# A graph layer on one core: the second layer's results turned by VectorE, another read order for the edges, shifted tables, five more picks

## The chip, the cores and the metric

The kernel runs on one core of a Trainium2 chip. The metric is the device time of one execution in microseconds (us). Before the change three runs took 1513.1 (median), 1511.35 and 1513.92 us. A separate execution was recorded by the profiler; all durations below come from it.

## The reference

There are 6250 nodes with 64 features each, and 200000 edges sorted by their target `dst`. For every edge a small network makes nine weights from 32 attributes; they scale nine further attributes, and the source node's features are combined with them. The results are summed per target node, scaled and shifted by a function of `node_vec`, added to `x`, and normalised.

```python
w = jax.nn.silu(edge_attr @ W1 + b1) @ W2 + b2
h_src = features[src]
msg = jnp.einsum('ef,em,fmg->eg', h_src, edge_sh * w, W_tp)
agg = jax.ops.segment_sum(msg, dst, num_segments=N) / jnp.sqrt(jnp.float32(AVG_DEG))
emb = jax.nn.silu(c_noise[:, None] @ Wn1 + bn1) @ Wn2 + bn2
gamma, beta = jnp.split(emb, 2, axis=-1)
return agg * (1.0 + gamma) + beta
```

The final step is `_layernorm(x + ...)` over the 64 features.

## The kernel before

**Tiling.** The edges stand in 1563 tiles of 128, one edge per partition, and in 98 groups of 16 tiles (`KB`; the last has 11). Because the edges are sorted, the 128 edges of a tile reach at most 7 neighbouring nodes (`W`). A fallback for other inputs stands behind the main path and is not run.

**Three ways to fetch the source rows.** The features of an edge's source node go into a tile `hs` of the group, and come from one of three places. Most tiles are fetched by an indirect DMA that GpSimd issues (`gather`, L99), one per tile. The last 3 or 4 tiles of each group are "picked" by TensorE. One tile of each fourth group is read row by row by DMAs of the SP queue (L115). That makes 1173 gathers, 367 picks and 23 tiles by rows.

**A pick** (`pick`, L488 to L511) works on a copy of the whole node table in SBUF, split in two parts of reduced precision: `xs[0]`, rounded, and `xs[1]`, the remainder. Node number 49 p + 7 h + l lies on partition p. For each h, VectorE compares the edges' keys with the partition numbers (`hots`, L485); the one-hot matrix `hot_k[:, h, :]` is the weight operand of two matmuls, one for each part of `xs` (L500, 448 columns: 64 features by 7 values of l). Fourteen of them add up in `px`, a PSUM tile with two buffers. VectorE then keeps the right l (L509, `xm`) and adds over l (L511) into `hs`. A pick can begin only when L509 of the pick before the last has read the buffer it is to use. How many picks a group has is set by `picked`: 4, or 3 where the group's number is a multiple of 4.

**The edge network.** `hidden` (L423) multiplies the attributes by `W1` in two matmuls of 512 columns (L428) into the PSUM tile `p1`, 64 hidden values for two sets of edges on 128 partitions; ScalarE applies silu (L436). `second` (L440) multiplies by `W2` in four matmuls (L445), one for each 128 columns, each into its own 32 partitions of the PSUM tile `p2`; ScalarE adds the bias into `p2s` (L448). There, the weights lie along partitions and the edges along the columns. `weights` (L450) turns this: two TensorE transposes of 128 by 128 (L455), put back into `p2`, then two multiplications by the nine attributes (L461), and one by the one-hots of the target within its window of 7 (L467), which makes `a`.

**Sums.** `windows` (L519) multiplies `hs` and `a` for every tile (L533): 64 features by 9 times 7 sums. Its first matmul in a group waits for all gathers of the group. `project` (L565) multiplies by `W_tp` for two groups at a time (L579); ScalarE copies the result to `rt` (L582), and TensorE turns it (L585); ScalarE and VectorE split it (L553, L554) and VectorE makes place marks (L563). `place` and `bring` (L595, L612) put the sums to their nodes, and `finish` normalises and stores 2 x 128 nodes at a time.

**Order.** It is written out by hand; each engine executes in the program's order. Iteration i issues the gathers of group i + 6, the first pick of group i + 1 with the node work of `nodes` between its matmuls, then `hidden(i + 2)`, `second(i + 1)`, `windows(i)`, `project` in odd iterations, and the rest of the picks. The second pick carries other work between its matmuls: after each pair of matmuls, `pick` calls the next entry of a list, which is built at L675 from `weights(i + 1)` (two entries) and, in odd iterations, from `project` (two empty entries and the turn, L585). `hs` has seven buffers.

**Addresses.** The tiles are laid out in the order in which they are made. Helper `even` rounds small tiles up to 128 bytes, so that all large tiles start at multiples of 64 bytes in a partition. `xs[0]`, `xs[1]` and all one-hot tiles start at multiples of 256.

Of the kernel before, what the change touches and what calls it, by code (L numbers as in the profile page):

```python
# [11 lines left out]
F32R = mybir.dt.float32r  # L12
# [4 lines left out]
P = 128  # L17
N, F, M, D, H, E = 6250, 64, 9, 32, 64, 200000
NJ = 49
# [10 lines left out]
Q = 4  # L30
J = 7
# [19 lines left out]

def picked(g):

    return Q - (g % 4 == 0)


def tiles(g):
# [3 lines left out]
def even(pool, p, n, dt, **kw):  # L61

    per = 32
    return pool.tile([p, -(-n // per) * per], dt, **kw)[:, 0:n]
# [3 lines left out]
def gnn_resnorm_kernel(ctx: ExitStack, tc: tile.TileContext, x, src, dst, dst_row, ea, sh, cn,  # L68
                       w1, b1, w2, b2, wtp, wn1, bn1, wn2, bn2, out):
    nc = tc.nc  # L70
# [6 lines left out]
    w1bd = consts.tile([P, 2 * H], F32)  # L77
# [9 lines left out]
    with ExitStack() as fast:  # L87
# [3 lines left out]
        keep = fast.enter_context(tc.tile_pool(name="keep", bufs=1))  # L91
# [5 lines left out]
        def gather(g):  # L97
            hs[g] = gath.tile([P, KB, F], F32, tag="hs", name=f"hs{g}")
            hs_dma[g] = [nc.gpsimd.indirect_dma_start(  # L99
                out=hs[g][:, t - g * KB, :], out_offset=None, in_=x,  # L100
                in_offset=bass.IndirectOffsetOnAxis(ap=src_i[:, t:t + 1], axis=0))
                for t in range(g * KB + (g in SPG), g * KB + tiles(g) - picked(g))]
# [14 lines left out]
        ident = keep.tile([P, P], F32)  # L117
        ident2 = keep.tile([P, F], F32)
        w2p = keep.tile([P, D], F32)
        b2c = even(keep, P, 1, F32, name="b2c")  # L120
        xs = [keep.tile([P, J, F, J], F32R, name=f"xs{i}") for i in range(2)]
        wi = even(keep, P, W, F32, name="wi")
        nf = keep.tile([P, 2 * P], F32)
        lo = even(keep, P, NBLK, F32, name="lo")
# [20 lines left out]
        def setup(temp):  # L145
# [77 lines left out]
            def keys_first(g, kf, tag):  # L223

                pk_t[g] = psum.tile([P, Q, P], F32, tag=tag, name=f"pk{g}")
                for t in range(picked(g)):
                    c = (g + 1) * Q - picked(g) + t
                    d0 = NBLK * KB + c * P
                    dg = xb.rearrange("p j f -> p (j f)")[:, d0:d0 + P]
                    nc.vector.tensor_scalar(dg, ident, kf[:, c:c + 1], None, op0=ALU.mult)  # L230
                    nc.tensor.matmul(pk_t[g][:, t, :], ones, dg, start=True, stop=True)  # L231
# [26 lines left out]
            pick(0, 0)  # L258
            hots(0, 2, Q)
            hidden(0)  # L260
            keys_first(1, kf, "s")
            hots(1, 0, 1)
# [4 lines left out]
            hots(1, 1, Q)  # L267
            second(0)
            pick(0, 2, [[lambda: None, lambda: None], weights(0)])
            hidden(1)  # L270

            nc.sync.dma_start(dst_i[:, 2 * KB:], dst[:, 2 * KB:])
# [150 lines left out]
        def hidden(g, act=True):  # L423

            e = ea_t.pop(g)
            p1 = psum.tile([P, 2, KB * P // 4], F32, tag="p1", name=f"p1_{g}")
            for i in range(2):
                nc.tensor.matmul(p1[:, i, :], w1bd[i * 64:(i + 1) * 64, :], e[i * 64:(i + 1) * 64, :],  # L428
                                 start=True, stop=True)
            p1_t[g] = p1  # L430
            if act:
                hidden_act(g)

        def hidden_act(g):
            st[g] = work.tile([P, 2, KB * P // 4], F32, tag="st", name=f"st{g}")
            nc.scalar.activation(st[g], p1_t.pop(g), AF.Silu, bias=b1c)  # L436
# [13 lines left out]
        def weights(g):  # L450

            p, v = p2.pop(g), p2s.pop(g)

            def part(i):
                nc.tensor.transpose(p[:, 1, i * P:(i + 1) * P], v[:, i * P:(i + 1) * P], ident)  # L455
                if i == 0:
                    return
                sw = p[:, 0, 0:KB * M].rearrange("p (t m) -> p t m", m=M)
                sh = sh_t.pop(g)
                for i in range(2):  # L460
                    nc.vector.tensor_mul(  # L461
                        sw[:, 8 * i:8 * i + 8].rearrange("p (s c) m -> p s c m", s=2),
                        p[:, 1, i * P:(i + 1) * P].rearrange("p (c q) -> p c q", q=D)[:, :, 0:2 * M]
                        .rearrange("p c (s m) -> p s c m", s=2),
                        sh[:, 8 * i:8 * i + 8].rearrange("p (s c) m -> p s c m", s=2))
                a[g] = work.tile([P, KB, M, W], F32, tag="a", name=f"a{g}")
                nc.vector.tensor_mul(a[g], oh_t.pop(g)[:, :, None, :].to_broadcast([P, KB, M, W]),  # L467
                                     sw.unsqueeze(3).to_broadcast([P, KB, M, W]))

            return [lambda i=i: part(i) for i in range(2)]  # L470

        hot_k = {}

# [162 lines left out]
        with tc.manual_schedule(), tc.tile_pool(name="temp", bufs=1) as temp:  # L636
            setup(temp)

            for i in range(NBLK):
# [26 lines left out]
                if i + 2 < NBLK:  # L666
                    hidden(i + 2)
# [5 lines left out]
                if i % 4 == 1 and i - 1 < NJ:  # L673
                    gate_hidden(i - 1)
                pick(i + 1, 1, [weights(i + 1), turn])  # L675
                for t in range(2, Q):
                    pick(i + 1, t)

            g = NBLK - 1
            second(g)  # L680
            nc.scalar.activation(root, eps, AF.Sqrt)
            pick(g, 1, [weights(g)])
            pick(g, 2)
            sums(g)
# [225 lines left out]
```

## Time and profile before

| What | Value |
|---|---|
| Median of three runs | 1513.1 us |
| Profiled execution, whole | 1512.09 us |
| Span from its first to its last instruction | 1510.2 us |
| TensorE busy | 1459.4 us (97%) |
| VectorE busy | 1152.7 us (76%) |
| ScalarE busy | 514.6 us (34%) |
| GpSimd busy | 1113.2 us (74%) |
| DMA | 96.3 MB, 64 GB/s on average |

A line of the groups reads: source line, engine, operation, the tiles written and read, their shapes, how many; then busy time in total and mean duration of one in ns; then the idle time of that engine just before them, and who ended most of it. Matmuls overlap in the array and their ends are modelled, so a mean duration of 374 ns does not say how far apart they follow each other; their start times do. A line of the timeline reads: start and duration in us, engine, line, operation, tiles, and in brackets the idle time before it with the one who ended it. PE is TensorE, PEld its weight loads, DVE VectorE, ACT ScalarE, POOL GpSimd, SP the engine that issues most DMAs.

### The profile page before, as it was taken

How to read it: one execution, taken by the hardware profiler on the slowest of the kernel's cores; microseconds unless marked ns; L12 is line 12 of the kernel's file. 1: busy time of each engine (PE TensorE's matmuls, PEld its weight loads, DVE VectorE, ACT ScalarE, POOL GpSimd, SP SyncE). 2: the span in 40 equal slices, each digit the busy share in tenths (PEclk: the TensorE clock that was granted, in tenths of full speed). 3: DMA queues.
4: the chain of work that ended last, by engine and by line, in shares of the span. 5: the costliest groups of instructions: out<-in, count | busy, mean ns of one | idle time of the engine just before them, and what ended most of it. 6: DMA issues, size and time to landing. Idle time of an engine off the chain costs nothing.

```text
span 1510.2 us, 34381 instructions
## 1 busy us (share of the span) xinstructions
PE 1459.4 (97%) x10984; PEld 1207.7 (80%) x10984; DVE 1152.7 (76%) x2044; ACT 514.6 (34%) x1326; POOL 1113.2 (74%) x1182
## 2 busy tenths in 40 slices
PE   5899999999999999999999999999999999999996
PEld 3688788878787888787878888788888888888885
DVE  6777877777868777778687788777886877877774
ACT  3333333333423333334233333243342333333342
POOL 7777777777777777777777777777777777777770
PEclk9899999999999999999999999999999999999997
DMA  5422222222222222222222222222222222222210
GB/s 166 97 72 64 72 58 64 55 59 70 65 57 73 58 64 54 69 61 65 54 73 54 60 54 73 60 55 54 71 62 54 72 55 60 70 58 60 72 30 7
DMA packets 90424, 96.30 MB, mean 64 GB/s; under 512 B 36824, under 2 KB 51370, under 8 KB 90234
## 3 DMA queue, kind: packets, MB, share of 16 engines
q1 hardware_dynamic: 52122, 53.89, 12.0%
q0 software_dynamic: 37536, 38.51, 11.6%
q8 instruction: 90, 1.47, 0.4%
q10 hardware_dynamic: 576, 1.61, 0.3%
q14 instruction: 100, 0.82, 0.2%
HBM read 92.17 MB, written 1.73 MB: 62 GB/s over the span
## 4 chain that ended last, share of the span: by engine, by line
PE 84%; DVE 6%; ACT 2%; issue 2%; SPq 2%; POOL 2%; DMA 1%; DVEq 0%; POOLq 0%; ACTq 0%
PE px L500 63%; PE pz L533 6%; PE p L428 5%; PE p L445 3%; PE pt L579 3%; POOL hs L99 2%; SPq L115 1%; PE p L455 1%; ACT L436 1%; DMA hs<-in_x_dram,src_i 1%; ACT st L436 1%; DVE xm L509 1%; PE ps L595 1%; DVE hs L511 1%; PE ps L625 1%
## 5 line engine op out<-in xcount | busy, mean ns | idle before, releaser
L99 POOL DMA_INDIRECT hs<-in_x_dram,src_i x1173 | 1111.9, 948 | 359.5 <-issue 316.9
L500 PE MATMUL px<-xs,hot_k 128*128 128x448 f32 x5138 | 1136.1, 374 | 2.0 <-ACT xs L245 1.3
L500 PEld LDWEIGHTS px<-xs,hot_k 128*128 128x128 f32 x5138 | 929.7, 189 | 93.5 <-DVE xs L246 3.2
L509 DVE SCALAR_TENSOR_TENSOR xm<-li,jl,px 128x448 f32<-128x448 f32 x367 | 248.3, 677 | 231.7 <-PE px L500 231.7
L485 DVE TENSOR_TENSOR hot_k<-pk,nk 128x896 fp32r<-128x896 f32 x367 | 382.7, 1081 | 1.9 <-PE pk L231 1.9
L436 ACT ACTIVATE st<-p,b1c 128x1024 f32<-128x1024 f32 x98 | 109.1, 1114 | 399.6 <-PE p L428 399.3
L511 DVE TENSOR_REDUCE hs<-xm 128x64 f32<-128x448 f32 x367 | 227.6, 620 | 12.6
L543 ACT COPY ztw<-pz 64x140 f32<-64x140 f32 (+1 forms) x780 | 208.6, 267 | 16.5 <-PE pz L533 5.3
L533 PEld LDWEIGHTS pz<-a,hs 128*64 128x64 f32 x3116 | 100.0, 138 | 43.5 <-issue 42.7
L467 DVE TENSOR_TENSOR a<-oh,p 128x1008 f32<-128x1008 f32 x98 | 118.0, 1204 | 3.3
L533 PE MATMUL pz<-a,hs 128*64 128x63 f32 x3116 | 113.4, 225 | 3.0 <-issue 2.0
L428 PE MATMUL p<-ea,w1bd 64*128 64x512 f32 x392 | 111.6, 646 | 0.0
L601 ACT COPY carry<-ps 128x128 f32<-128x128 f32 x48 | 12.8, 266 | 277.2 <-PE ps L595 277.2
L461 DVE TENSOR_TENSOR p<-p,sh 128x72 f32<-128x72 f32 x196 | 47.0, 240 | 59.1 <-PE p L455 27.4
L445 PEld LDWEIGHTS p<-st,w2p 128*32 128x32 f32 x784 | 15.8, 108 | 89.3 <-issue 43.9
L728 ACT ACTIVATE var<-var,eps 128x2 f32<-128x2 f32 (+1 forms) x25 | 7.4, 295 | 207.5 <-DVE var L725 207.5
L445 PE MATMUL p<-st,w2p 128*32 128x256 f32 x784 | 63.1, 393 | 15.4 <-DVE xb L369 7.9
L579 PE MATMUL pt<-ztw,wtc 128*64 128x112 f32 x960 | 55.3, 261 | 2.7 <-ACT st L436 2.5
L479 ACT CAST pk<-kr 128x512 f32<-128x512 f16 (+1 forms) x96 | 54.2, 564 | 1.7 <-DMA kr<-kd 1.7
L455 PE MATMUL p<-ident,p2s 128*128 128x128 f32 x196 | 53.5, 273 | 0.1
L428 PEld LDWEIGHTS p<-ea,w1bd 64*128 64x128 f32 x392 | 29.7, 186 | 29.8 <-issue 26.4
L579 PEld LDWEIGHTS pt<-ztw,wtc 128*64 128x64 f32 x960 | 46.8, 137 | 4.6 <-ACT st L436 4.0
(139 smaller groups left out, 528.5 us busy)
## 6 DMA issues: line engine op xcount, KB each, us to landing
hs<-in_x_dram SPq DMA_DIRECT2D x2944, 0.2 KB
ea<-in_ea_dram SPq DMA_DIRECT2D x48, 512.0 KB
hs<-in_x_dram,src_i POOLq DMA_INDIRECT x1173
kr<-kd SPq DMA_DIRECT2D x48, 256.0 KB
sh<-in_sh_dram SPq DMA_DIRECT2D x49, 144.0 KB
cb<-cn_d SPq DMA_DIRECT2D x12, 128.0 KB
out_dram<-o SPq DMA_DIRECT2D x24, 64.0 KB
dst_i<-in_dst_dram SPq DMA_DIRECT2D x1, 768.0 KB
```

The lines of the kernel that those rows point to most:

```text
L99: hs_dma[g] = [nc.gpsimd.indirect_dma_start(out=hs[g][:, t - g * KB, :], out_offset=None, in_=x, in_offset=bass.IndirectOffsetOnAxis(ap=sr ...
L428: nc.tensor.matmul(p1[:, i, :], w1bd[i * 64:(i + 1) * 64, :], e[i * 64:(i + 1) * 64, :], start=True, stop=True)
L436: nc.scalar.activation(st[g], p1_t.pop(g), AF.Silu, bias=b1c)
L445: nc.tensor.matmul(p2[g][c * D:(c + 1) * D, 0, :].rearrange("p (i e) -> p i e", i=2), w2p, s[:, :, c * P:(c + 1) * P], start=True, stop=True)
L467: nc.vector.tensor_mul(a[g], oh_t.pop(g)[:, :, None, :].to_broadcast([P, KB, M, W]), sw.unsqueeze(3).to_broadcast([P, KB, M, W]))
L485: nc.vector.tensor_tensor(hot_k[g, t], pk_t[g][:, t, None, :].to_broadcast([P, J, P]), nk.unsqueeze(2).to_broadcast([P, J, P]), op=ALU.is_ ...
L500: nc.tensor.matmul(px.rearrange("p f l -> p (f l)"), hot_k[g, t][:, h, :], xs[i][:, h].rearrange("p f l -> p (f l)"), start=(h == 0 and i ...
L509: nc.vector.scalar_tensor_tensor(xm, li[:, None, :].to_broadcast([P, F, J]), jl[:, c:c + 1], px, op0=ALU.is_equal, op1=ALU.mult)
L511: nc.vector.tensor_reduce(hs[g][:, tiles(g) - q + t, :], xm, AX.X, ALU.add)
L533: mm = nc.tensor.matmul(pz[v][v * F:(v + 1) * F, k // 2].rearrange("p m w -> p (m w)"), hsg[:, k0 + k, :], ag[:, k0 + k].rearrange("p m w ...
L543: nc.scalar.copy(z[h * F:(h + 1) * F, 0:5 - h, k0 + v:k0 + n:2, :].rearrange("p m k w -> p k m w"), pz[v][v * F:(v + 1) * F, 0:(n + 1 - v) ...
L579: nc.tensor.matmul(pt[h * F:(h + 1) * F, 0, 0:KW], wtc2[:, c, :], z[h][:, c], start=(c == 0), stop=(c == 4))
```

## The change

It has four parts.

- The two TensorE transposes of a group are replaced by one VectorE transpose, which turns each 32 by 32 block of the 128 by 256 tile by itself. The list of `weights` so has one entry instead of two.
- Block-wise turning leaves an edge in the quarter of the partitions in which its block lay. So that the edges still come out in their places, the first layer reads its 512 columns in another order: its four sets of 128 are read by quarters of 32, first quarters first.
- `xs` becomes one tile with both parts in it, each with a margin of 32 bytes in front. In the built program the parts start at 139296 and 151968, the one-hots at 190976 and every 3584 bytes on.
- `picked` gives 3 picks where the group's number is a multiple of 5: 20 groups instead of 25. There are 372 picks and 1168 gathers.

```diff
 def picked(g):
 
-    return Q - (g % 4 == 0)
+    return Q - (g % 5 == 0)
...
-        xs = [keep.tile([P, J, F, J], F32R, name=f"xs{i}") for i in range(2)]
+        xs_w = keep.tile([P, 2, NJ * F + 32], F32R)
+        xs = [xs_w[:, i, 8:8 + NJ * F].rearrange("p (h f l) -> p h f l", h=J, f=F) for i in range(2)]
...
             for i in range(2):
-                nc.tensor.matmul(p1[:, i, :], w1bd[i * 64:(i + 1) * 64, :], e[i * 64:(i + 1) * 64, :],
+                nc.tensor.matmul(p1[:, i, :].rearrange("p (c t e) -> p c t e", c=4, t=4), w1bd[i * 64:(i + 1) * 64, :],
+                                 e[i * 64:(i + 1) * 64, :].rearrange("p (t c e) -> p c t e", t=4, c=4),
                                  start=True, stop=True)
...
-            def part(i):
-                nc.tensor.transpose(p[:, 1, i * P:(i + 1) * P], v[:, i * P:(i + 1) * P], ident)
-                if i == 0:
-                    return
+            def part():
+                nc.vector.transpose(p[:, 1, :], v)
                 sw = p[:, 0, 0:KB * M].rearrange("p (t m) -> p t m", m=M)
...
-            return [lambda i=i: part(i) for i in range(2)]
+            return [part]
```

## The prediction

> **What bounds the kernel now.** I read the busy times first, then the chain that ended last, then the costliest groups.
>
> ```profile
> PE 1459.4 (97%) x10984; PEld 1207.7 (80%) x10984; DVE 1152.7 (76%) x2044; ACT 514.6 (34%) x1326; POOL 1113.2 (74%) x1182
> ...
> PE 84%; DVE 6%; ACT 2%; issue 2%; SPq 2%; POOL 2%; DMA 1%; DVEq 0%; POOLq 0%; ACTq 0%
> ...
> L99 POOL DMA_INDIRECT hs<-in_x_dram,src_i x1173 | 1111.9, 948 | 359.5 <-issue 316.9
> L500 PE MATMUL px<-xs,hot_k 128*128 128x448 f32 x5138 | 1136.1, 374 | 2.0 <-ACT xs L245 1.3
> ...
> L455 PE MATMUL p<-ident,p2s 128*128 128x128 f32 x196 | 53.5, 273 | 0.1
> ```
>
> TensorE carries 84% of the chain and waits for almost nothing. GpSimd looks idle for a quarter of the span, but 316.9 us of that is "issue": it waits for nobody. The timeline from 1451 us shows what this means.
>
> ```profile
> 1451.62 1.15 PE L533 MATMUL pz<-a,hs 128*64 128x63 f32 x32
> ...
> 1452.38 0.94 POOL L99 DMA_INDIRECT hs<-in_x_dram,src_i  x1 [0.30 <-issue]
> ...
> 1453.21 0.27 PE L455 MATMUL p<-ident,p2s 128*128 128x128 f32 x1
> ...
> 1453.63 0.94 POOL L99 DMA_INDIRECT hs<-in_x_dram,src_i  x1 [0.31 <-issue]
> 1453.73 0.27 PE L455 MATMUL p<-ident,p2s 128*128 128x128 f32 x1
> ...
> 1454.11 0.52 DVE L461 TENSOR_TENSOR p<-p,sh 128x72 f32<-128x72 f32 x2 [1.01 <-PE p L455]
> 1454.66 1.20 DVE L467 TENSOR_TENSOR a<-oh,p 128x1008 f32<-128x1008 f32 x1
> ...
> 1466.52 1.15 PE L533 MATMUL pz<-a,hs 128*64 128x63 f32 x32
> ...
> 1472.36 0.94 POOL L99 DMA_INDIRECT hs<-in_x_dram,src_i  x1 [0.30 <-issue]
> ```
>
> Gathers follow each other every 1.247 us, without a break from about 50 us until the last, 1173rd, one at 1472.36. So there are two chains: TensorE's work, and 1173 gathers in a row. They meet at L533, whose first matmul needs its group's gathers. Group 95's L533 starts at 1466.52; groups 96 and 97 have 13 + 7 gathers, so group 95's last gather ended near 1448.3: TensorE came 18 us later than the gathers. That margin was 30 us at the start and shrank after 800 us.
>
> Two sizes come from start times in the trace. A pick without other work between its 14 matmuls has 13 intervals of 2634 ns in all: 202.6 ns each. A second pick of an odd group, with two L455 transposes inside, has 2960. Its first interval is 311 instead of 203 because it follows L533's small matmuls; that 108 is not the transposes'. They cost 2960 - 2634 - 108 = 218 ns, 109 each. Check: where L585 is added, 3080, so 120 for one more transpose. The 273 ns of the row overlap neighbours.
>
> **What the Trainium skill says.** TensorE: Matmul & The Clock Gate, "Back-to-back issue gap", gives columns / 2.4 + 2.5 ns: 189.2 for 448 columns. The trace, with a granted clock of 1.00 in every stretch from 50 to 1480 us, has 202.6: 13.4 ns more. SBUF — State Buffer, "Who interferes with whom", says that TensorE has two independent read ports, for moving operand and weights, and waits for nobody. It speaks against a gain from addresses, but does not explain the 13.4. Vector Engine (DVE) Microarchitecture Reference, 3.8, says that the block transpose sustains one element per cycle per lane; no transpose of VectorE is in this trace.
>
> **The change, part by part.**
>
> (a) 196 transposes and their weight loads leave TensorE: 98 x 0.218 = -21.4 us on the path.
>
> (b) 98 block transposes come to VectorE. Its rows cost about 156 ns + 1.06 per element (L721: 292 for 128, 224 for 64), so an estimate of 0.43 us, 42 us in all; were each block filled and drained in turn, 0.7. Lower bound is half the elements' time, 0.29. What hides it: VectorE idles 24% of the span, and its waits before L461 (59.1 us) go, 27.4 of them for L455. The tight place is the second pick of every fourth group: there L509 frees its px buffer 0.91 us (median) before TensorE wants it. Minus 0.218 and 0.43 leaves 0.26. Queued behind are the two L461, L467, L554, the marks and L509; the next pick but one waits for L509. Cost 0; at 0.7 still about 0 to 1 us, and 24 x the excess beyond.
>
> (c) The list given to the second pick loses one entry, so L585 comes after 8 matmuls, not 10 matmuls and two transposes: 0.62 us earlier. Its weight load now starts 0.55 to 0.57 us after the copy of rt ended in 12 of 48 cases, 0.78 or more in nearly all others. With 0.06 for the semaphore (L554's end to L595 near the end) about 12 waits of 0.12: +1.5. ACT's copy and VectorE's L554 and marks follow it, earlier than before.
>
> (d) 25 groups had three picks, now 20: five more. TensorE 5 x 14 x 0.2026 = +14.2. VectorE 5 x (1081 + 677 + 620) ns = 12, hidden in idle. GpSimd loses 5 gathers: -6.2 on its own chain, 4 of them (-5.0) by group 95.
>
> (e) L428 reads 16 runs of 32 columns (128 bytes each). No row before does so; L445 reads two runs of 128 at no visible cost. I take 0. Bounds: -1 (no mechanism for more), and +10, at four lost cycles (1.7 ns) for each run in two passes of two matmuls per group: 64 x 1.7 x 98.
>
> (f) In the built program the two xs start at 139264 and 151808 per partition, one-hots at 190720 and every 3584 on, rows inside step by 1792 and 512: both streams always start at a multiple of 256. After: 139296 and 151968 against 190976: always 32 past a multiple of 128. It concerns 372 x 14 = 5208 matmuls, 5.2 us per ns. Bounds: -13.4 ns (the whole excess, -70 us), and on the other side, which no row excludes, as much. The excess is about the same for L595 (256 columns, 119 ns against 109.2), so it goes with the matmul and its 128-column weight load, not with columns: what two colliding reads of the same weights would give. Against it: L579, also at multiples of 64, needs 48 ns for 112 columns per pass, almost no excess, though with 64 weight columns.
>
> **The sum.** TensorE without (f): 1510.2 - 21.4 + 14.2 + 1.5 = 1504.5. GpSimd: group 95's gathers end at 1443.3, land 1.1 to 2.4 later, so L533 can start at 1444.8; TensorE without (f) is there at 1466.5 - 96 x 0.218 (20.9) + 4 x 2.84 (11.3) + 1.5 = 1458.4. The 13.6 between is all that (f) can give: 2.7 ns per matmul, a fifth of the excess. Beyond that, from 1444.8 on: 1510.2 - 1466.5 = 43.7 as before, + 2.8 for group 96's new pick, - 0.4 for two groups' transposes, - 0.3: 1490.6. A span shorter by 19.6. The profiled execution took 1512.1, 1.9 around its span; the median of runs is 1513.1, so 1493.5.
>
> **The cases.** A, 55%: (f) gives 2.7 ns or more, GpSimd's chain sets the end: 1493.5 (1491 to 1496). For it: four fifths of the interval between no gain and the whole excess lie here. B, 14%: a gain below 2.7 ns, which TensorE passes on whole, 5.2 us per ns: 1496 to 1506, 1500.4 at half. C, 18%: the offset does nothing, as the two ports suggest, and one part of the change does not do what it says: 1504.5 + 2.9 = 1507.4, still 5.7 faster. GpSimd then keeps 13.6 us of margin and never shows. D, 13%, the other side: the reads from xs become slower at the new offset. Nothing in the trace speaks for it but that no matmul of this shape was seen there. It decides from 5.7 / 5.2 = 1.1 ns; at 5 ns the time is 1533. I drop VectorE as the bound: it would need 0.26 us beyond 0.43 in one block, and then costs 24 x the rest.
>
> The range 1489.5 to 1508.5 holds A, B and C but for their edges, some 82%; A's own is 1491 to 1496. Less than 0.2% (3 us) can't be told from no change. A, B and C are faster, (e) at its upper bound takes C to the same, D splits: faster 0.86, same 0.05, slower 0.09.
>
> **What would show it.** L500's interval: 200 or less for A, 202.6 for C, above 203.7 for D. L533 waiting for hs gathers at groups 75 to 95, in A only. Last gather near 1466. No L455; VectorE's transpose at 0.43. L428 at 527 ns per matmul. L585's weight load waiting for ACT some 0.1 us. The forecast is wrong if gathers lose their pace of 1.247, if L509 comes late every block, or if the interval doesn't move.

## The result and the profile after

The changed kernel takes 1510.76 us (median of 12 runs, 1508.88 to 1511.82 us); the kernel before, run beside it, 1512.76 (12 runs, 1510.41 to 1514.67). The ratio is 0.9989, with a 95% interval of 0.9980 to 0.9997: 0.5 to 3 us faster, which the prediction's own bound of 0.2% does not tell from no change. 1493.5 was forecast, and 1510.8 lies above the range. The profiled execution has a span of 1507.1 us, 3.1 shorter than before.

From the page of the changed kernel: the busy times, the chain that ended last, and the groups that answer to those shown of before.

```profile
PE 1456.1 (97%) x10858; PEld 1204.8 (80%) x10858; DVE 1202.3 (80%) x2157; ACT 515.3 (34%) x1326; POOL 1108.4 (74%) x1177
...
PE 86%; DVE 6%; SPq 2%; issue 2%; ACT 2%; DMA 1%; POOL 1%; DVEq 0%; POOLq 0%; ACTq 0%
...
L99 POOL DMA_INDIRECT hs<-in_x_dram,src_i x1168 | 1107.2, 948 | 358.0 <-issue 317.2
L500 PE MATMUL px<-xs_w,hot_k 128*128 128x448 f32 x5208 | 1133.0, 371 | 2.4 <-ACT xs_w L246 1.3
...
L461 DVE TENSOR_TENSOR p<-p,sh 128x72 f32<-128x72 f32 x196 | 47.3, 241 | 6.7
```

L455 is gone and 126 matmuls are fewer (196 transposes less, 70 of five more picks), VectorE is busy for 50 us more, and TensorE still fills 97% of the span and carries 86% of the chain. The gathers are five fewer and just as fast. The timeline of the changed kernel at group 44's windows (L533) and the second and third picks of group 45 shows the new order.

```profile
712.24 1.15 PE L533 MATMUL pz<-a,hs 128*64 128x63 f32 x32
...
713.32 6.38 PE L500 MATMUL px<-xs_w,hot_k 128*128 128x448 f32 x30
...
715.08 0.45 DVE L457 STREAM_TRANSPOSE p<-p2s 128x256 f32<-128x256 f32 x1
...
715.56 0.52 DVE L461 TENSOR_TENSOR p<-p,sh 128x72 f32<-128x72 f32 x2
...
717.24 0.67 DVE L509 SCALAR_TENSOR_TENSOR xm<-li,jl,px 128x448 f32<-128x448 f32 x1
```

TensorE now goes through the second pick without a break, and one block transpose of 0.45 us on VectorE stands where two of TensorE stood. The same timeline near the end:

```profile
1461.68 1.15 PE L533 MATMUL pz<-a,hs 128*64 128x63 f32 x32
...
1466.18 0.94 POOL L99 DMA_INDIRECT hs<-in_x_dram,src_i  x1 [0.30 <-issue]
```

Group 95's L533 starts at 1461.7, where its gathers had ended at 1443.4 (96 and 97 take 12 + 7 after them). The margin is still 18 us, so the gathers bound nothing. The forecast had TensorE there at 1444.8.

Where the time went is in the start times of L500 in the trace. The table gives the sum of the 13 intervals between the 14 matmuls of a pick; the first row is a pick without other work in it, and the two others are second picks, which carry the transposes:

```
                        before   after
13 intervals of a pick    2634    2645 ns   (202.6 -> 203.5 per matmul)
second pick, odd group    2960    2761 ns   (-199 = -210 + 11)
second pick, with L585    3080    2873 ns   (-207 = -218 + 11)
```

The matmuls after alternate between 205 ns (with xs part 0) and 202 (part 1). 5208 matmuls x 0.85 ns = 4.4 us. So the sum is -20.5 (96 second picks, freed of the offset's 11 ns) + 14.2 (five picks) + 4.4 = -1.9 us, and the medians show -2.0. That they agree to 0.1 us is luck in part, because single executions differ by more. In the traces the changed kernel is 2.0 us ahead at group 1 (64.4 against 66.4), where f1 below, with the same instructions on other addresses, is at 66.6. And at group 60 TensorE waits once for VectorE, 2.94 us in the kernel before and 3.01 in the changed one. The changed kernel's trace shows a granted clock of 0.50 for the next 3.4 us, where the kernel before has 1.00, and it loses some 1.2 us.

In eleven of the eighteen runs below (e1 to e5, g1 to g4, h5 to h7) TensorE was held at half its clock for long stretches (the kernel before took 2442 to 2533 us beside them), so only their intervals at full clock are read, and no times.

### The profile page after: what moved, and what is told of

Same layout as the page of the kernel before. It is cut to its first block, busy times and chain, and to the rows that moved or that the text cites. A ratio compares the mean times of both kernels' runs of the same rounds, so it can differ in the third digit from the quotient of the medians.

```text
span 1507.1 us, 34188 instructions
## 1 busy us (share of the span) xinstructions
PE 1456.1 (97%) x10858; PEld 1204.8 (80%) x10858; DVE 1202.3 (80%) x2157; ACT 515.3 (34%) x1326; POOL 1108.4 (74%) x1177
## 4 chain that ended last, share of the span: by engine, by line
PE 86%; DVE 6%; SPq 2%; issue 2%; ACT 2%; DMA 1%; POOL 1%; DVEq 0%; POOLq 0%; ACTq 0%
PE px L500 66%; PE pz L533 6%; PE p L429 5%; PE p L447 3%; PE pt L579 3%; SPq L115 2%; DMA hs<-in_x_dram,src_i 1%; PE ps L595 1%; DVE xm L509 1%; ACT L438 1%; PE ps L625 1%; POOL hs L99 1%; ACT st L438 1%; DVE hs L511 1%; DVE hot_k L485 1%
## 5 line engine op out<-in xcount | busy, mean ns | idle before, releaser
L500 PE MATMUL px<-xs_w,hot_k 128*128 128x448 f32 x5208 | 1133.0, 371 | 2.4 <-ACT xs_w L246 1.3
L500 PEld LDWEIGHTS px<-xs_w,hot_k 128*128 128x128 f32 x5208 | 954.4, 188 | 95.4 <-DVE xs_w L247 3.4
L509 DVE SCALAR_TENSOR_TENSOR xm<-li,jl,px 128x448 f32<-128x448 f32 x372 | 251.6, 676 | 221.6 <-PE px L500 219.1
L485 DVE TENSOR_TENSOR hot_k<-pk,nk 128x896 fp32r<-128x896 f32 x372 | 387.6, 1081 | 2.1 <-PE pk L232 2.1
L511 DVE TENSOR_REDUCE hs<-xm 128x64 f32<-128x448 f32 x372 | 230.7, 620 | 12.8
L533 PEld LDWEIGHTS pz<-a,hs 128*64 128x64 f32 x3116 | 100.8, 139 | 44.0 <-issue 39.4
L533 PE MATMUL pz<-a,hs 128*64 128x63 f32 x3116 | 114.2, 226 | 3.2 <-issue 2.4
L429 PE MATMUL p<-ea,w1bd 64*128 64x512 f32 x392 | 110.6, 641 | 0.0
L447 PEld LDWEIGHTS p<-st,w2p 128*32 128x32 f32 x784 | 15.8, 108 | 89.2 <-issue 44.7
L447 PE MATMUL p<-st,w2p 128*32 128x256 f32 x784 | 63.3, 395 | 15.2 <-DVE xb L370 7.6
L579 PE MATMUL pt<-ztw,wtc 128*64 128x112 f32 x960 | 55.2, 261 | 2.4 <-ACT st L438 1.8
L429 PEld LDWEIGHTS p<-ea,w1bd 64*128 64x128 f32 x392 | 29.5, 184 | 30.1 <-issue 26.0
L450 ACT ACTIVATE p2s<-p,b2c 128x256 f32<-128x256 f32 x98 | 45.7, 466 | 15.6 <-PE p L447 15.6
L579 PEld LDWEIGHTS pt<-ztw,wtc 128*64 128x64 f32 x960 | 46.8, 137 | 4.3 <-ACT st L438 3.0
```

The costliest lines, as they stand in the source:

```text
L429: nc.tensor.matmul(p1[:, i, :].rearrange("p (c t e) -> p c t e", c=4, t=4), w1bd[i * 64:(i + 1) * 64, :], e[i * 64:(i + 1) * 64, :].rearra ...
L447: nc.tensor.matmul(p2[g][c * D:(c + 1) * D, 0, :].rearrange("p (i e) -> p i e", i=2), w2p, s[:, :, c * P:(c + 1) * P], start=True, stop=True)
L485: nc.vector.tensor_tensor(hot_k[g, t], pk_t[g][:, t, None, :].to_broadcast([P, J, P]), nk.unsqueeze(2).to_broadcast([P, J, P]), op=ALU.is_ ...
L500: nc.tensor.matmul(px.rearrange("p f l -> p (f l)"), hot_k[g, t][:, h, :], xs[i][:, h].rearrange("p f l -> p (f l)"), start=(h == 0 and i ...
L509: nc.vector.scalar_tensor_tensor(xm, li[:, None, :].to_broadcast([P, F, J]), jl[:, c:c + 1], px, op0=ALU.is_equal, op1=ALU.mult)
L511: nc.vector.tensor_reduce(hs[g][:, tiles(g) - q + t, :], xm, AX.X, ALU.add)
```

## The experiments

**The offset apart from the rest.** The first four runs put the xs back to the start of the shared tile, or took the layout or the picks alone:

```diff
 e1: -xs_w[:, i, 8:8 + NJ * F]      +xs_w[:, i, 0:NJ * F]          (changed kernel, 372 picks)
 e3: e1 and  -Q - (g % 5 == 0)      +Q - (g % 4 == 0)              (367 picks)
 e4: kernel before,  -(g % 4 == 0)  +(g % 5 == 0)                  (372 picks alone)
 e5: kernel before with xs_w and the slice 8:8 + NJ * F             (offset alone)
```

> The changed kernel with the two node tables back at a multiple of 256 bytes (the first at the tile's start, the second 12672 bytes on); all else as changed. Theory O (the 32 bytes cost): the pick's 13 intervals fall from 2645 back to 2634 ns, 0.85 ns per matmul, 5208 x 0.85 = 4.4 us less than the changed kernel: about 1506.4, 0.4% under the kernel before. Rival V (the offset does nothing; the longer interval comes from VectorE's new work or anything else in the change): 2645 ns stay and the time is that of the changed kernel, 1510.8.

> As the run with offset 0, and with 3 picks in groups that are a multiple of 4 again: 367 picks, 1173 gathers, transposes on VectorE. TensorE alone would be done after 1510.2 - 98 x 0.21 = 1490 us of span (median some 1492). Theory G (GpSimd's row of gathers becomes the bound once TensorE gives back more than about 15 us): L533 waits for gathers from about group 91 on, span 1494.7, median about 1497. Rival to G (gathers don't bind): 1492, no waits for gathers. Under theory V add 4 us to the TensorE figures: 1494 of span, where G and its rival would not differ.

> The kernel before with 372 picks and nothing else. A pick costs TensorE 14 x 202.6 ns = 2.84 us, five cost 14.2: 1527 us. If the picks were partly hidden by something that TensorE waits for, less: down to 1513.

> The kernel before with the node tables 32 bytes further on and nothing else. Theory O: the pick's 13 intervals go from 2634 to 2645 ns, 5138 x 0.85 = 4.4 us more: 1517.1. Rival V: 2634 and 1512.8. If the offset gained in this kernel (the idea of the forecast), 1512.8 less 5.1 us per ns.

The 13 intervals of a third pick of an odd group took, in ns:

```
before                       2631          e4 (372 picks)        2630 to 2635
changed kernel               2645          e5 (offset alone)     2645
e1 (slice at 0)              2641 to 2645 or 2657 to 2660
e3 (slice at 0, 367)         2641 to 2645 or 2656 to 2660
```

e5 has the changed kernel's number and its 205/202 pattern with TensorE's transposes still in place: the layout makes the 0.85 ns, not the transposes, the order of L429 or the picks. But e1 did not come back to 2631. In the shared tile the parts lie 12,672 bytes apart, not 12,544, so "slice at 0" isn't the layout of before: the second part starts 128 bytes past a multiple of 256. Only the two original tiles give that layout back.

**The original tiles, at both numbers of picks.**

```diff
-        xs_w = keep.tile([P, 2, NJ * F + 32], F32R)
-        xs = [xs_w[:, i, 8:8 + NJ * F].rearrange("p (h f l) -> p h f l", h=J, f=F) for i in range(2)]
+        xs = [keep.tile([P, J, F, J], F32R, name=f"xs{i}") for i in range(2)]
 f2 also:
-    return Q - (g % 5 == 0)
+    return Q - (g % 4 == 0)
 f3, in the place of that:
+    return {88: 4, 92: 4, 96: 2, 97: 3}.get(g, Q - (g % 4 == 0))
```

> The changed kernel with the two original xs tiles (starts at 139264 and 151808, one-hots at 190720), all else of the change kept, 372 picks. Theory O (the 32-byte offset costs 0.85 ns per matmul of a pick): interval of clean picks back to 202.6 ns, 5208 x 0.85 = 4.4 us less than the changed kernel, about 1506.3 us median where the kernel before has 1512.8, ratio near 0.996. Rival V (the offset does nothing to the sum, the change's transposes gave less than 20 us): interval 202.6 to 203.5, time as the changed kernel, 1510.8, ratio 0.999.

> As f1_two_tiles_372, but with the picks of the kernel before (367): what is left of the change are the transposes on VectorE and the first layer's reads in another order. If only TensorE counted: before - 20.5 = 1492.3 us. Theory G (the chain of 1173 gathers becomes the bound when TensorE gives back more than about 15 us): L533 waits for gathers from a group between 85 and 93 on, in three or four groups, up to 1.7 us each, about 5 us in all, 1497 us, ratio 0.990; last gather at 1472 as before. Rival: the transposes are worth less than 15 us and no L533 waits, 1498 or more.

> As f2_two_tiles_367 with the same number of picks laid out otherwise: groups 88 and 92 have four, 96 has two, 97 three, so two fewer gathers stand ahead of groups 88 to 95 and two more behind. Theory G: the gather chain still has 1173 links and ends at the same time, but the waits at groups 88 to 93 are nearly gone, 1492.5 to 1494 us, ratio 0.987, 3 to 5 us under f2_two_tiles_367. If gathers do not bind in f2_two_tiles_367, this one has the same time as it within 1 us.

f1: 1508.84 us, ratio 0.9981 (0.9972 to 0.9989). f2: 1496.35, ratio 0.9895 (0.9879 to 0.9910). f3: 1497.94, ratio 0.9904 (0.9888 to 0.9919). The kernel before took 1512.21 beside them.

f1 and f2 differ by five picks and 12.5 us. At group 95's L533 (L532 in these two kernels), where no end effect enters, f1 is at 1463.3 and f2 at 1451.7: 11.6 for four picks, 2.9 each, as the forecast priced them. So the five picks eat most of what the transposes give.

But f1 is not where theory O had it: its median is 1.9 us under the changed kernel's, not 4.4, and their ratios overlap, though the third picks of its even groups are back at 2630 to 2635. The chain of waits of f2 (start, length, work; x44 is the run of full matmuls in picks 2 to 4 of an odd group, from the L532 just before it to the next other matmul) shows why:

```profile
171.69 9.11 PE px L499 x44
202.02 9.29 PE px L499 x44
231.13 9.11 PE px L499 x44
261.45 9.29 PE px L499 x44
290.64 9.29 PE px L499 x44
...
588.47 9.11 PE px L499 x44
```

The same 44 matmuls take 9.11 or 9.29 us. In the trace the slow runs have 2687 ns per 13 intervals (206.7 each), the quick ones 2631 to 2638, and the first intervals of the second pick tell which it will be:

```
f2, group  5: 313 201 207 207 206 207 207 206 207 207 206 207 207   slow, through picks 2, 3 and 4
f2, group  9: 307 198 208 202 203 202 199 207 203 202 203 199 206   quick, through picks 2, 3 and 4
before, g. 7: 313 234 284 228 286 195 200 206 203 202 203 199 207   quick; two transposes among the first six
```

In f1, f2 and f3 together all 50 odd groups whose first interval was 312 to 314 ns were slow, and none of the 94 at 306 to 310 (the other three, two of them slow, started at 537 or 538, right after the wait at group 60). The third picks of even groups are never slow after group 2, and of their fourth picks only a few in f1: there a transpose comes among the matmuls of the second pick (L584 in these three, L585 in the kernel before). In the kernel before 24 odd groups started with 313 or 314, in e4 30 more, and none was slow: there L455 came between. This gave theory L: a run of full matmuls falls into a rhythm that its start decides, and keeps it until another kind of matmul comes between. The transposes that the change removes had also been the interruption.

Theory L also accounts for f1 on TensorE. The old tiles save 4.4 us and its 20 slow groups give back 0.18 us each, 3.6. From group 1 to group 95 its trace gains 0.6 us on the changed kernel's.

**Is it the weight load?** The prediction had taken the 13.4 ns above 189.2 for a matter of the 128-column weight load. In f4 the middle twelve matmuls of a pick load only the first 64 one-hot columns, so half of the picked rows lack most of their products and are wrong; the run is there for its intervals.

```diff
+                    n = P if (h == 0 and i == 0) or (h == J - 1 and i == 1) else P // 2
-                    nc.tensor.matmul(px.rearrange(...), hot_k[g, t][:, h, :],
+                    nc.tensor.matmul(px[0:n].rearrange(...), hot_k[g, t][:, h, 0:n],
```

> As f1_two_tiles_372, but of the 14 matmuls of a pick the middle 12 have only the first 64 of the 128 one-hot columns as weights, so half of the rows of px get two products out of 14 and those picked rows are wrong. Theory W (the 13.4 ns[...] go with the 128-column weight load of each matmul): interval of the middle matmuls 188 to 197 ns; TensorE then gives back 372 x 11 x 6 to 13 ns = 25 to 53 us on top, the gather chain (1168 links) sets the end, near 1490 us whatever the interval, with L533 waiting for gathers in many groups. Rival: the excess is per matmul and independent of the weights' width, interval 202.6, time as f1_two_tiles_372.

1505.61 us, ratio 0.9956 (0.9941 to 0.9971). From its page, the matmuls and their weight loads:

```profile
L500 PE MATMUL px<-xs,hot_k 128*64 128x448 f32 (+1 forms) x5208 | 1126.5, 370 | 2.6 <-ACT xs L245 1.3
L500 PEld LDWEIGHTS px<-xs,hot_k 128*64 128x64 f32 (+1 forms) x5208 | 725.0, 143 | 306.7 <-DVE xs L246 4.4
```

and from that of f1:

```profile
L499 PE MATMUL px<-xs,hot_k 128*128 128x448 f32 x5208 | 1134.1, 372 | 2.4 <-ACT xs L245 1.3
L499 PEld LDWEIGHTS px<-xs,hot_k 128*128 128x128 f32 x5208 | 957.5, 189 | 93.9 <-DVE xs L246 3.4
```

The mean load falls from 189 to 143 ns, and the pick stays at 2633 ns, 202.5 per matmul. The excess doesn't come from the load's length: theory W falls. What f4 gains on f1 fits theory L: each of its picks mixes two shapes of matmul, 43 of its odd groups start with 313 or 314, and none is slow.

**Breaking the rhythm, and other offsets.**

```diff
 g1 (on f1), g4 (on f1, with 368 picks: group 92 keeps four):
+    for f0, f1 in [(0, F // 2), (F // 2, F)] if (g % 2, t, h, i) == (1, 1, 1, 0) else [(0, F)]:
+        nc.tensor.matmul(px[:, f0:f1]..., hot_k[g, t][:, h, :], xs[i][:, h, f0:f1]..., ...)
 g2 (changed kernel):   -(g % 5 == 0)        +(g % 4 == 0)
 g3 (changed kernel):   -8:8 + NJ * F        +16:16 + NJ * F
```

> As f1_two_tiles_372, but in the second pick of every odd group the third matmul is given as two of 224 columns with the same weights. Theory L (a run of full matmuls falls into a rhythm that its start decides and keeps it until another kind of matmul comes between; in f1_two_tiles_372 the odd groups whose first interval is 312 ns or more keep 206.7 ns through picks 2 to 4, and without TensorE's transposes nothing breaks it): after the split pair the rhythm is found anew, no odd group at 206.7, picks 3 and 4 of all odd groups at 2631 to 2638 ns; 20 groups x 40 intervals x 4.1 ns = 3.3 us less, 49 x about 20 ns = 1 us more for the extra matmul, so 1506.5 us where f1_two_tiles_372 had 1508.8, ratio 0.9965. Rival M (odd groups are slowed by other work of theirs, on VectorE or the queues): a third of the odd groups stay at 2687, time 1509 to 1510.

> The changed kernel, 32-byte offset and all, with the 367 picks of the kernel before. Theory L: the offset makes every run of matmuls fall into 205/202 in turn, mean 203.5, whatever its start; 5138 x 0.9 ns = 4.6 us, as much as the slow odd groups cost f2_two_tiles_367. Then group 95's L533 starts within 2 us of f2_two_tiles_367's 1451.7, and the time is 1496 to 1498 us, ratio 0.990. If instead the offset costs on top of the slow groups: 1500 or more, ratio 0.9925.

> The changed kernel with the xs slices 64 bytes instead of 32 into the shared tile, 372 picks. If the rhythm depends on where the two xs parts lie to each other (spacing 12672 bytes here as with 32, 12544 in the kernel before): 205/202 as in the changed kernel, 1510.8, ratio 0.999. If it depends on the 32 bytes themselves (half of 64): another rhythm, 202.5 to 203.0 with or without slow odd groups, 1506 to 1509, ratio 0.9955 to 0.998.

> As g1_split_372 with 368 picks: those of the kernel before and a fourth for group 92, so 1172 gathers. Theory L and theory G together: without slow groups TensorE alone would end at 1489.8 + 2.8 + 1 = 1493.6 (span), the gathers let group 97 start at 1472.3 + 1.3 and end the kernel near 1492.5; 1493 to 1494 span, 1495 to 1496 median, ratio 0.989, 0 to 1.5 us under f2_two_tiles_367. Theory M: TensorE 3 us later, 1498 to 1499.

In g1 all 49 third picks of odd groups are at 2630 to 2638 ns and none at 2687 (20 in f1), though 16 of these groups started with 313 or 314. Splitting one matmul in two is enough; rival M falls. g4: 46 quick and 3 slow; in these three the first interval is 537 or 538, and the clock rose from half to full only behind the split pair, which could not break what began after it. g2: 2641 to 2650 in third picks. g3: 2636 to 2641, a rhythm of its own at 203.0. Each offset has a rhythm, and at 32 bytes (g2, h2, e5, h5) and 64 (g3) none of 21 starts at 312 to 314 led to a slow one.

**Three of them again, for their times.**

> The kernel of g1_split_372 on an undisturbed chip. Theory L: no slow odd groups, 3.3 us less than f1_two_tiles_372, and about 1 us more for 49 extra matmuls: 1506.5 us, ratio 0.9965 to the kernel before. Rival M (what slowed the odd groups was another cost that the split pair does not remove from the sum): as f1_two_tiles_372, 1508.8 to 1510, ratio 0.998 to 0.9985.

> The kernel of g2_off32_367 on an undisturbed chip: the transposes moved, the offset, 367 picks. Theory L: 5138 x 0.9 = 4.6 us for the 205/202 rhythm in the place of about 4 us of slow groups: 1496 to 1498 us, ratio 0.990, L533 of group 95 within 2 us of 1451.7. If the offset costs on top: 1500 or more.

> The kernel of g4_split_368 on an undisturbed chip: transposes on VectorE, no offset, split pair, 368 picks. Theory L with the gathers: 1495 to 1496 us, ratio 0.989, 0 to 1.5 us under f2_two_tiles_367. Theory M: 1498 to 1499, ratio 0.991.

h1: 1509.26 us, ratio 0.9972 (0.9960 to 0.9983). h2: 1499.53, ratio 0.9909 (0.9892 to 0.9925). h4: 1500.99, ratio 0.9919 (0.9905 to 0.9933). The kernel before took 1512.28.

h1 has no slow group left, with 18 starts at 313 or 314; its L533 of group 95 starts at 1461.7 where f1 had 1463.3. That is 1.5 us of the 2.3 expected net. It would be 2.6, but after the wait at group 60 h1's clock stays at 0.50 for 6.8 us, f1's for 3.4, and h1 loses 1.1 us more there. The two ratios overlap and 1509.26 lies in rival M's range, so the time alone doesn't decide between L and M; the intervals do. In h2 the chain of waits has one length for all runs of 44:

```profile
171.57 9.15 PE px L500 x44
...
201.96 9.15 PE px L500 x44
231.02 9.15 PE px L500 x44
261.41 9.15 PE px L500 x44
290.57 9.15 PE px L500 x44
```

At group 80's L533 h2 is at 1232.5 and f2 at 1234.0; the 1.5 us between them are the half clock after group 60, which h2 was spared. So on TensorE the offset costs as much as the slow groups that it replaces. Yet h2's median is 3.2 us above f2's (the two sets of times don't meet, the intervals of the ratios do), and h4 is 5 us above what was expected. h2's timeline at group 88 shows what holds it:

```profile
1345.95 0.94 POOL L99 DMA_INDIRECT hs<-in_x_dram,src_i  x1 [0.30 <-issue]
...
1347.69 0.64 PE L447 MATMUL p<-st,w2p 128*32 128x256 f32 x8
...
1348.70 1.15 PE L533 MATMUL pz<-a,hs 128*64 128x63 f32 x32 [0.37 <-DMA hs<-in_x_dram,src_i]
```

The group's last gather is issued at 1345.95, and its landing releases L533 at 1348.70. From the start of L447's last matmul to that of L533 it takes 0.31 us normally; in h2 groups 88, 89, 90, 92 and 93 take 0.44 to 1.05 more, 3.5 us in all, and in h4 groups 84 to 90 together 4.4. This is the meeting of the two chains that the forecast's case A described, at the groups that it named. It only needed TensorE to be 13 us earlier there than in the changed kernel (1348.7 against 1361.9).

f2 just escapes. Its L532 comes 1.9 to 2.6 us after the last gather's end at groups 92 to 94, and at none of groups 48 to 95 does it come later than the usual 0.31 us after L446: slow groups had kept its TensorE 3 us back (17 times 0.18), and its gathers followed each other every 1.2512 us (from the 200th on), where h2's took 1.2533 and h4's 1.2540, 2 to 3 us over the chain. This pace is not the kernel's own. f3 is the same program as f2 up to group 87 and ran on the same chip, and its gathers took 1.2532 and were 2.2 us later at group 80. So f2's escape is in part that of one execution; whether the other three had waits was not recorded. Theory G missed for f2, whose 1497 was met by way of the slow groups and not by waits, and holds for h2 and h4. f3 has 6 to 9 us of margin at groups 88 to 95, as it was made to have, and is still no faster. Its timeline of TensorE at the end:

```profile
1473.07 1.15 PE L532 MATMUL pz<-a,hs 128*64 128x63 f32 x32
1474.05 0.36 PE L578 MATMUL pt<-ztw,wtc 128*64 128x112 f32 x2
1476.08 1.08 PE L578 MATMUL pt<-ztw,wtc 128*64 128x112 f32 x17 [1.67 <-ACT ztw L542]
```

and that of f2:

```profile
1469.63 1.15 PE L532 MATMUL pz<-a,hs 128*64 128x63 f32 x32
1470.71 3.10 PE L499 MATMUL px<-xs,hot_k 128*128 128x448 f32 x14
1473.74 1.18 PE L578 MATMUL pt<-ztw,wtc 128*64 128x112 f32 x20
```

In f2 group 97's fourth pick stands between the windows of group 96 and their projection, and covers ScalarE's copies (L542). f3 had taken that pick away, and TensorE waits for the copies. This wait was in nobody's expectation.

**Three last runs** were to price the offset and the picks alone, and to run f2 once more.

> The kernel before with the shared xs tile and its 32-byte offset as the only edit, on an undisturbed chip. Theory L: all picks in the 205/202 rhythm, 5138 x 0.85 = 4.4 us more, 1516.7 where the kernel before has 1512.3, ratio 1.0029. Rival V (the offset costs no time): ratio 1.000.

> The kernel before with 372 picks as the only edit. As predicted: 5 x 2.84 = 14.2 us more, 1526.5, ratio 1.0094; gathers keep 25 us or more of margin.

> The kernel of f2_two_tiles_367 once more. If its lead is its own: ratio 0.9895 again, 1496.3. If the gathers' pace of a run decides: last gather between 1473 and 1477, the end 20 to 22 us behind it, 1495.5 to 1499.5, ratio 0.989 to 0.991.

The rhythms repeat in third picks: h5 2645 in every odd group; h7, in odd groups, a mixture of 19 at 2687 and 30 at 2630 to 2635; h6 2630 to 2639, but for four groups at 2687 (14, 54, 71 and 76). So slow groups belong to the kernel and not to one run. But h6 and h7 also bound theory L. Two slow groups of h7 had started with 308. And h6 has all its transposes: in its groups 14 and 54 the clock was full, and the slow rhythm began right behind L585. An interruption lets the rhythm be found anew, and nearly always, not always, it is the quick one. The offset's 4.4 us alone, as a time, was not measured.

## Why the prediction was wrong

Wrong by 17 us, and by one step, (f), with the case A that was built on it.

**(f), the offset: wrong.** The forecast put 55% on a gain of 2.7 ns or more and measured is a loss of 0.85 ns, 4.4 us. The bounds of 13.4 ns to either side hold, but the step then spread its chance over the gain's side and counted four fifths of that interval as an argument. No row of the profile spoke for a gain. The Trainium skill (SBUF — State Buffer, "Who interferes with whom"), by which TensorE has two independent read ports, spoke against it. Of the operands' addresses, which did change the interval here, that section says nothing. The 13.4 ns were also no gap that this stream was known to be able to close: the Trainium skill (TensorE: Matmul & The Clock Gate, "Back-to-back issue gap") gives its formula for a single isolated matmul, and here the interval of a stream was held against it. The step then laid the excess to the 128-column weight load, against L579, which has almost none with 64 columns. f4 shows that the width is not the cause: with 64 columns the interval is the same. So reads of the weights that collide in proportion to their number are not what the 13.4 ns are. What they are stays open. With (f) at nothing the working gave 1507.4, case C; with the measured 4.4 and without the 1.5 of (c) it gives 1510.3, and 1510.8 was measured. (f) was the one step that decided: case A needed 13.6 us from it and it took 4.4.

**(a), the transposes: right for the second pick, with something missing.** 0.199 and 0.207 us came off, 0.210 and 0.218 without the offset's 11 ns, for 0.218. The 108 ns of the first interval were rightly left to L533: it is still 310. What the step didn't see is that the transposes broke up the run of matmuls. Without them and without the offset 15 to 20 of the 49 odd groups fall into a rhythm of 206.7 ns and give back 0.18 us each, 3 us in f2. In the changed kernel the offset prevents this, at 0.85 ns on all. Net, f1 against the changed kernel, the offset costs between nothing and 2 us (0.6 in the traces), where (f) on its own term is 4.4.

**(b), VectorE: right.** The transpose takes 0.45 us for 0.43; in the tight place L509 still frees its buffer 0.28 us (median) before TensorE wants it, 0.26 was forecast. VectorE's 50 us more are hidden.

**(c), L585 earlier: the wait right, its price wrong.** In exactly 12 of 48 cases its weight load now starts only 0.05 us after the copy of rt ends, and the load stream stands idle 0.11 to 0.13 us before it, not 0.02. But the matmuls hardly feel it: those second picks take 2870 to 2883 ns, the other 35 2860 to 2875. A wait on the weight load is not yet a wait of the train, and the 1.5 us didn't come.

**(d), five picks: right.** 2.9 us each on TensorE, and group 95's gathers end at 1443.4 for 1443.3. (One gather takes 1.250 us on average from the 200th on, not 1.247.)

**(e), the scattered read: right.** L429's matmuls come in pairs 6 or 7 ns apart, and the next pair follows after 526 or 527 ns, as L428's did before.

**The gathers' floor: right, but not reached by the changed kernel.** The waits appear in h2 and h4, with 367 and 368 picks, at groups 84 to 93; with 372 TensorE leaves 18 us.

The lowest median of these kernels is f2's, with the transposes on VectorE, the old tiles and the old picks: 1496.35 us, 1.05% under the kernel before. The intervals don't tell it from f3 and h2.

## What to carry to other kernels

Where a step has no row in the profile, its bounds say how wrong one can be, not which side is likely; a chance of 55% shouldn't be read off the width of a gap in knowledge. When an instruction is taken out of a long train of equal matmuls, measure the train's interval again on both sides of it, not only the place where it stood: what was removed may have set the train's rhythm. And with two chains some 15 us apart, a gain on one is worth its full size only up to that margin, and a trade that moves work between them (a pick for a gather) is best set anew once the gain is measured.

## What was new about the hardware

The interval of back-to-back fp32r matmuls of 448 columns with new 128-column weights each takes one of several values at full clock: 202.5, 203.0 (xs 64 bytes into the shared tile), 203.5 (32 bytes), 203.3 or 204.5 (e1's layout) or 206.7 ns. Which one depends on where the operands lie and, with the old tiles, on how the run starts: with 312 to 314 ns for the first interval all 50 were slow, with 306 to 310 none of 94 (in h7 two were). It is then kept for 42 matmuls, until a matmul of another shape comes between, which nearly always brings the quick one back. The Trainium skill (TensorE: Matmul & The Clock Gate, "Back-to-back issue gap") gives 189.2 by its formula for an isolated matmul, and no layout tried here came near it; halving the weight columns, and with them the load from 188 to 135 ns, changed nothing.

A block transpose of 128x256 fp32 from SBUF to PSUM on VectorE takes 0.45 us (436 to 460 ns). At group 60 pauses of TensorE of 3.01 to 3.15 us were followed by a granted clock of 0.50 for 3.4 us or, in h1, 6.8 in seven traces (after, f1 to f4, h1, h4); pauses of 2.94 (before) and 3.01 us (h2) were not.

Why a start falls on 313 rather than 309, and why in f1 to f3 and h7 slow groups end by group 73, was not found.
